# Column sums of the second weight from rows added on GpSimd, and three held steps instead of two at the end of a feed-forward layer

## The chip, the cores and the metric

The kernel runs on one core of a Trainium2 chip. The metric is device time in microseconds (us); lower is better. Engines are named as in the profile: PE (TensorE, matrix products), DVE (VectorE), ACT (ScalarE), POOL (GpSimd) and SP (SyncE, which issues the DMAs).

## The reference

One transformer block for 4 samples of 512 tokens with 512 features. Cross-attention with 32 heads of 16 comes first, then a feed-forward layer whose weights are reduced to three values (-g, 0, g):

```python
x = x + attention(layernorm(x), ctx, ...) @ Wout + bout
def bitlinear(x, w):                       # forward values only
    return einsum('bsd,od->bso', layer_norm(x), sign(round(w / (g + EPS))) * g)   # g = mean(|w|)
h = gelu(bitlinear(layernorm(x), w_fc))    # 512 -> 2048
x = x + bitlinear(h, w_proj)               # 2048 -> 512
```

(The activation quantization changes the value by rounding only.) The second `bitlinear` normalizes each row of `h` before the product. The kernel does it the other way round: it multiplies the unnormalized `h` by the signs W and corrects afterwards. With m the mean and r the inverse deviation of a token's row of `h`,

out = x + r g (h W - m (column sums of W)).

So it needs the column sums of W, one row of 512 numbers: the sum of W over its 2048 rows.

## The kernel before, in words

**Attention** takes the first two thirds of the time. It ends with the last head groups of sample 3. For every second group, a block of 128 rows of `aT` (the attention output) is fetched, and then multiplied on POOL by reciprocals `rb` that went through DRAM (L523, `spread`). The sign chunks of W lie in DRAM; the last four head groups each free two buffers, into which `load_second` (L612) loads two pieces of 256 rows of W. In the end `wproj_sb[f]`, f = 0 to 15, is W as 16 tiles of 128 rows by 512 columns.

**Feed-forward** has 64 steps (sample b, block f of 128 hidden features). The loop over n (L1034) writes the order out by hand for PE, DVE and ACT; POOL and SP are not in that set (L1017), so a scheduler places their instructions. In step n:

- `first(b, f)`, L923: 8 products (4 blocks of features, in a high and a low part) into `hp`, then ACT's Gelu gives `h`.
- `split(b, f)`, L938: ACT rounds `h` to `hh` (L942) and squares it (L953); DVE adds `h` to a running sum (L955), forms the low part `hl` (L956) and adds the squares (L957). All three DVE additions read two tiles of SBUF.
- In steps 6 to 9 of sample 0, the output projection `op` of one tile of 128 tokens of sample 3 (L1047): four products, one for each block k of `aT`.
- In step 7, `column_sums` (L974): 16 products with a matrix of ones (`ones_r`), one for each `wproj_sb[f]`, accumulate the column sums; ACT copies them to `wsum`.
- `second(b, f, t)`, L960, for the four tiles t of 128 tokens, two steps behind `first`: each is a product with `hh` and one with `hl`, 8 in a step.

After the last step of a sample, `totals` (L981) makes 8 small products of the running sums with ones, and a chain of two DVE and six POOL instructions turns them into m and r. For each tile of tokens `centered` (L1003, DVE) subtracts m times the column sums, and `finish` (L1010, DVE) scales by r, adds x and stores.

**The end.** The last two steps of sample 3 are held back: their products are not made step by step but tile by tile (L1096). For t = 0: its 4 products, then `totals`, then `centered(0)`. For t = 1, 2, 3: 4 products, `centered(t)`, `finish(t-1)`. At last `finish(3)`.

Tiles of the feed-forward stage come from `fpool`, opened when attention's pools are closed, so they lie where attention's tiles were, and their first writer waits until those are no longer used.

Of the kernel before, what the change touches and what calls it, by code (L numbers as in the profile page):

```python
# [9 lines left out]
F32 = mybir.dt.float32  # L10
F32R = mybir.dt.float32r
AF = mybir.ActivationFunctionType
ALU = mybir.AluOpType
AX = mybir.AxisListType

P = 128
# [15 lines left out]
def xattn_ffn(  # L32
# [13 lines left out]
    nc = tc.nc  # L46
    B, S, D = x.shape
# [4 lines left out]
    KD, KC, KF = D // P, C // P, F // P  # L52
# [189 lines left out]
    def run(k, end=0):  # L242
        for f in later[end].pop(k, []):
            f()
# [365 lines left out]
    wproj_sb = {}  # L610
# [142 lines left out]
    def when(i, u=0):  # L753
        return burst_of["s", i * NU + u]

    def prepared(b, ready):
        yield [tokens(b, t, ready) for t in range(NT)] + [
            heads(b, n, w) for n in range(2) for w in "kq"
        ] + [values(b, t) for t in range(NT)]
        yield [heads(b, 2, w) for w in "kq"]  # L760
        yield [heads(b, 3, w) for w in "kq"]
# [6 lines left out]
    a, c2, c3 = prepared(2, when(NG))  # L768
    op = projections(0)
    queue += a + op[:2] + c2 + op[2:] + c3  # L770
    a, c2, c3 = prepared(3, when(2 * NG))
# [15 lines left out]
    for k, burst in enumerate(bursts):  # L787
# [72 lines left out]
        while True:  # L860
# [14 lines left out]
            left = open_chore.steps - open_chore.done  # L875
# [13 lines left out]
    left = sorted(later[0].keys() | later[1].keys())  # L889
# [6 lines left out]
    left = sorted(later[1])  # L896
# [13 lines left out]
    fpool = ctx.enter_context(tc.tile_pool(name="fpool", bufs=2))  # L910
# [4 lines left out]

    ones_r = fpool.tile([P, P], F32R, name="ones_r", bufs=1)
    wsum = fpool.tile([P, D], F32, name="wsum", bufs=1)
    hid, parts, acc, fin, outs, opre = {}, {}, {}, {}, {}, {}

    def xbank(name):  # L920
# [2 lines left out]
    def first(b, f):  # L923

        hp = ps_h.tile([P, S], F32, name=f"hp{b}_{f}", tag="h")
        for k in range(KD):
            for half in range(2):
                nc.tensor.matmul(  # L928
                    hp,
                    wfc_sb[k][:, f * P : (f + 1) * P],  # L930
                    dT[b][half][:, k, :],
                    start=half == 0 and k == 0,
                    stop=half == 1 and k == KD - 1,
                )
        hid[b, f] = fpool.tile([P, S], F32, name=f"h{b}_{f}", tag="h", bufs=3)
        nc.scalar.activation(hid[b, f], hp, AF.Gelu, scale=gam_fc[:, 0:1])  # L936

    def split(b, f):  # L938

        x = hid.pop((b, f))  # L940
        high = fpool.tile([P, S], F32R, name=f"hh{b}_{f}", tag="hh", bufs=UB)
        nc.scalar.copy(high, x)  # L942
        low = fpool.tile([P, S], F32R, name=f"hl{b}_{f}", tag="hl", bufs=UB)
        if f == 0:
            acc[b] = [
                fpool.tile([P, S], F32, name=f"acc{n}{b}", tag=f"acc{n}") for n in range(2)
            ]
            nc.scalar.activation(acc[b][1], x, AF.Square)
            nc.vector.tensor_tensor(low, x, high.bitcast(F32), ALU.subtract)
            acc[b].append(x)  # L950
        else:
            sq = fpool.tile([P, S], F32, name=f"sq{b}_{f}", tag="sq")
            nc.scalar.activation(sq, x, AF.Square)  # L953
            old = acc[b].pop() if f == 1 else acc[b][0]
            nc.vector.tensor_tensor(acc[b][0], old, x, ALU.add)  # L955
            nc.vector.tensor_tensor(low, x, high.bitcast(F32), ALU.subtract)  # L956
            nc.vector.tensor_tensor(acc[b][1], acc[b][1], sq, ALU.add)  # L957
        parts[b, f] = (high, low)
# [15 lines left out]
    def column_sums():  # L974

        p = ps_m.tile([P, D], F32, name="wsp", tag="m")
        for f in range(KF):
            nc.tensor.matmul(p, ones_r, wproj_sb[f], start=f == 0, stop=f == KF - 1)  # L978
        nc.scalar.copy(wsum, p)

    def totals(b):  # L981

        p = ps_m.tile([P, 2, NT], F32, name=f"tot{b}", tag="m")
        for n in range(2):
            for t in range(NT):
                nc.tensor.matmul(  # L986
                    p[:, n, t : t + 1],
                    acc[b][n][:, t * P : (t + 1) * P],
                    ones[:, 0:1],
                    start=True,  # L990
                    stop=True,
                )
        m = small.tile([P, 3, NT], F32, name=f"m{b}", tag="m")
        nc.vector.tensor_scalar(m[:, 0, :], p[:, 0, :], -1.0 / F, None, ALU.mult)
        nc.vector.tensor_scalar(m[:, 1, :], p[:, 1, :], 1.0 / F, None, ALU.mult)
        nc.gpsimd.tensor_tensor(m[:, 2, :], m[:, 0, :], m[:, 0, :], ALU.mult)
        nc.gpsimd.tensor_tensor(m[:, 1, :], m[:, 1, :], m[:, 2, :], ALU.subtract)
        nc.gpsimd.tensor_scalar(m[:, 1, :], m[:, 1, :], 0.0, None, ALU.max)  # L998
        r = rstd(m[:, 1, :], 1.0, EPS, NT, f"r_b{b}")
        nc.gpsimd.tensor_tensor(r, r, gam4, ALU.mult)  # L1000
        fin[b] = (m, r)
# [16 lines left out]
    with tc.manual_schedule(engines=ordered):  # L1018
        gam4 = small.tile([P, NT], F32, name="gam4", tag="gam4")
        nc.gpsimd.tensor_scalar(gam4, ones[:, 0:NT], gam_pr[:, 0:1], None, ALU.mult)  # L1020
        steps = [(b, f) for b in range(B) for f in range(KF)]
        todo = list(steps)
        after = {}
        ds = {}
        hold = 0

        def behind(n, f):
            after.setdefault(n, []).append(f)


        for n, s in enumerate(left[1:]):
            behind(2 + n, lambda s=s: run(s, 1))

        for n in range(len(steps) + 4):  # L1034
            on = n < len(steps)
            if on:
                b, f = steps[n]
                first(b, f)
                split(b, f)
                if f == KF - 1 and b + 1 < B:  # L1040
                    behind(n + 1, lambda b=b: totals(b))

            if on and b == 0 and 6 <= f < 6 + NT:
                t = f - 6
                p = xbank(f"op{B - 1}_{t}").rearrange("p k n -> p (k n)")
                for k in range(KD):
                    nc.tensor.matmul(  # L1047
                        p,
                        aT[B - 1][:, k, t * P : (t + 1) * P],
                        wout_sb[:, k, :],  # L1050
                        start=k == 0,
                        stop=k == KD - 1,
                    )
                i = (B - 1) * NT + t
                nc.vector.tensor_tensor(x_sb[:, i, :], p, x_sb[:, i, :], ALU.add)
            if on and b + 1 < B:
                at = (10, 11, 13, 14) if b == 0 else (6, 9, 12, 14)
                for t in range(NT):
                    i = (b + 1) * NT + t
                    if f == at[t] - 4:  # L1060
                        stats(i)
                    elif f == at[t] - 2:
                        ds[i] = prepare(i, fpool, "d")
                    elif f == at[t]:
                        first_T(i, ds.pop(i), xbank(f"tp_d{i}"))()
            if n == 3:
                nc.vector.tensor_copy(ones_r, ones)
            if n == 7:
                column_sums()
            count = 0  # L1070
            while todo and count < 2 and n >= hold:
                sb, sf = todo[0]
                m = sb * KF + sf
                if on and n - m < 2:
                    break
                if sb == B - 1 and sf >= KF - 2:
                    break
                todo.pop(0)
                count += 1
                for t in range(NT):  # L1080
                    second(sb, sf, t)
                if sf == KF - 1:
                    hold = n + 3
                    for t in range(NT):
                        behind(n, lambda b=sb, t=t: centered(b, t))
                        behind(n + 1 + t, lambda b=sb, t=t: finish(b, t))
                    break
            for x in after.pop(n, []):
                x()
            if not on and len(todo) == 2:  # L1090
                break
        for n in sorted(after):
            for x in after[n]:
                x()

        for t in range(NT):  # L1096
            for sb, sf in todo:
                second(sb, sf, t)
            if t == 0:
                totals(B - 1)  # L1100
            centered(B - 1, t)
            if t > 0:
                finish(B - 1, t - 1)
        finish(B - 1, NT - 1)
# [50 lines left out]
```

## Time and profile before

| | us |
|---|---|
| median of 6 runs (lowest to highest) | 857.15 (855.62 to 859.89) |
| the profiled execution: its own time | 857.86 |
| the profiled execution: span from first to last instruction | 856.1 |
| busy: PE, PE weight loads | 813.2, 430.2 |
| busy: DVE, ACT, POOL | 617.9, 456.6, 287.3 |
| mean granted PE clock | 0.991 of full speed |

How to read it: each row of a timeline gives the start, the duration, engine, line, operation, the tile written `<-` the tiles read, sizes and how many instructions were merged. In brackets stands how long the engine was idle before it, and what ended that wait. "PE L928 x8" in the chain of waits is 8 products of line 928 in a row. A column named PEclk is the share of full clock that PE was granted. Line numbers are those of the kernel before.

### The profile page before, as it was taken

How to read it: one execution, taken by the hardware profiler on the slowest of the kernel's cores; microseconds unless marked ns; L12 is line 12 of the kernel's file. 1: busy time of each engine (PE TensorE's matmuls, PEld its weight loads, DVE VectorE, ACT ScalarE, POOL GpSimd, SP SyncE). 2: the span in 40 equal slices, each digit the busy share in tenths (PEclk: the TensorE clock that was granted, in tenths of full speed). 3: DMA queues.
4: the chain of work that ended last, by engine and by line, in shares of the span. 5: the costliest groups of instructions: out<-in, count | busy, mean ns of one | idle time of the engine just before them, and what ended most of it. 6: DMA issues, size and time to landing. Idle time of an engine off the chain costs nothing. (4 is left out here: it accounts for less than half of the span.)

```text
span 856.1 us, 13868 instructions
## 1 busy us (share of the span) xinstructions
PE 813.2 (95%) x5364; PEld 430.2 (50%) x5364; DVE 617.9 (72%) x852; ACT 456.6 (53%) x603; POOL 287.3 (34%) x287
## 2 busy tenths in 40 slices
PE   4599999999999899999999999998999999999996
PEld 2123434344433333433333343336668888888885
DVE  4789878888887988878767877835455864864755
ACT  2245756566664546656555655576234544554442
POOL 3007375553833575577515731301000200100000
PEclk9799999999999999999999999999999999999998
DMA  6885867667596577867644667432000100100101
GB/s 188 280 324 167 264 230 246 219 206 239 196 303 207 184 248 237 293 211 261 210 149 167 230 210 271 150 126 100 1 1 0 50 1 1 50 0 1 50 1 49
DMA packets 75561, 135.25 MB, mean 158 GB/s; under 512 B 10728, under 2 KB 12648, under 8 KB 74984
## 3 DMA queue, kind: packets, MB, share of 16 engines
q1 hardware_dynamic: 75088, 133.72, 46.2%
q8 instruction: 42, 0.69, 0.3%
q10 hardware_dynamic: 408, 0.66, 0.2%
q14 instruction: 23, 0.19, 0.1%
HBM read 79.30 MB, written 55.05 MB: 157 GB/s over the span
## 5 line engine op out<-in xcount | busy, mean ns | idle before, releaser
L437 DVE TENSOR_REDUCE mx<-lp 128x2 f32<-128x1024 f32 x256 | 305.2, 1216 | 85.4 <-PE lp L423 84.6
L474 ACT ACTIVATE es<-sp 128x1024 f32<-128x1024 f32 x256 | 254.4, 1025 | 145.6 <-PE sp L470 137.5
L484 PE MATMUL av<-es,va 128*32 128x512 f32 x1024 | 136.0, 604 | 0.0
L462 PE MATMUL sp<-q_st,k_st 64*128 64x512 f32 x512 | 115.0, 446 | 8.3 <-DVE mx L437 7.5
L423 PE MATMUL lp<-k_st,q_st 64*128 64x512 f32 x512 | 112.7, 437 | 10.2 <-DMA q_st<-q_d 8.2
L936 ACT ACTIVATE h<-hp,gam_fc 128x512 f32<-128x512 f32 x64 | 44.0, 688 | 129.2 <-PE hp L928 129.2
L966 PE MATMUL fp<-wproj,hh 128*128 128x512 f32 x256 | 103.6, 405 | 0.0
L928 PE MATMUL hp<-dTh,wfc 128*128 128x512 f32 x256 | 100.5, 393 | 1.2 <-ACT dTh L657 1.2
L470 PE MATMUL sp<-mrows,sel 64*128 64x512 f32 x512 | 101.1, 391 | 0.2 <-ACT mrows L453 0.2
L966 PE MATMUL fp<-wproj,hl 128*128 128x512 f32 x256 | 101.2, 395 | 0.0
L928 PE MATMUL hp<-dTl,wfc 128*128 128x512 f32 x256 | 100.4, 392 | 0.2 <-DVE dTl L658 0.2
L955 DVE TENSOR_TENSOR acc<-acc,h 128x512 f32<-128x512 f32 x56 | 38.7, 691 | 73.5 <-ACT h L936 73.5
L462 PEld LDWEIGHTS sp<-q_st,k_st 64*128 64x128 f32 x512 | 48.0, 184 | 82.3 <-DVE mx L437 42.4
L423 PEld LDWEIGHTS lp<-k_st,q_st 64*128 64x128 f32 x512 | 48.2, 185 | 81.7 <-ACT es L474 40.9
L523 POOL TENSOR_TENSOR aT<-aT,rb 128x512 f32<-128x512 f32 x16 | 21.2, 1323 | 130.6 <-DMA rb<-rden_d 109.5
L285 PE MATMUL qpq<-xT,wq_sb 128*32 128x512 f32 x512 | 62.3, 594 | 0.7 <-ACT xT L321 0.7
L928 PEld LDWEIGHTS hp<-dTh,wfc 128*128 128x128 f32 x256 | 48.2, 188 | 12.6 <-ACT dTh L657 2.1
L966 PEld LDWEIGHTS fp<-wproj,hl 128*128 128x128 f32 x256 | 48.4, 189 | 11.2 <-issue 0.7
L966 PEld LDWEIGHTS fp<-wproj,hh 128*128 128x128 f32 x256 | 48.3, 189 | 11.2 <-issue 0.7
L928 PEld LDWEIGHTS hp<-dTl,wfc 128*128 128x128 f32 x256 | 48.1, 188 | 11.0 <-DVE dTl L658 0.5
L470 PEld LDWEIGHTS sp<-mrows,sel 64*128 64x128 f32 x512 | 48.4, 186 | 5.9 <-ACT mrows L453 0.8
L196 POOL TENSOR_SCALAR r_a<-mv 128x1 f32<-128x1 f32 x16 | 4.7, 292 | 130.3 <-DVE mv L633 130.3
(129 smaller groups left out, 1038.0 us busy)
## 6 DMA issues: line engine op xcount, KB each, us to landing
k_st<-k_d SPq DMA_DIRECT2D x32, 512.0 KB
q_st<-q_d SPq DMA_DIRECT2D x32, 512.0 KB
k_d<-sh_k SPq DMA_DIRECT2D x32, 256.0 KB
k_d<-sl_k SPq DMA_DIRECT2D x32, 256.0 KB
q_d<-sh_q SPq DMA_DIRECT2D x32, 256.0 KB
q_d<-sl_q SPq DMA_DIRECT2D x32, 256.0 KB
av_d<-avs SPq DMA_DIRECT2D x32, 256.0 KB
wm<-in_wfcT SPq DMA_DIRECT2D x16, 256.0 KB
```

What stands on the lines that cost most here:

```text
L285: nc.tensor.matmul(p[j * HP : (j + 1) * HP, :], w[:, j * HP : (j + 1) * HP], x, start=start, stop=stop,)
L423: nc.tensor.matmul(lp[:, h, :], q_st[i][rows, r, t * P : (t + 1) * P], k_st[i][rows, r, :], start=True, stop=True,)
L437: nc.vector.tensor_reduce(mx[i][:, t, :, r], lp, AX.X, ALU.max, negate=True)
L462: nc.tensor.matmul(sp[:, h, :], k_st[i][rows, r, c * P : (c + 1) * P], q_st[i][rows, r, :], start=True, stop=False,)
L470: nc.tensor.matmul(sp[:, h, :], sel[rows, r, :], mrows[i][rows, :], start=False, stop=True)
L474: nc.scalar.activation(es, sp, AF.Exp, scale=1.0 / math.sqrt(HD))
L484: nc.tensor.matmul(av[j * HP : (j + 1) * HP, :], va[b % 2][:, c, v0 : v0 + HP], es[r][:, h, :], start=c == 0, stop=c == NT - 1,)
L523: nc.gpsimd.tensor_tensor(aT[b][:, n, :], aT[b][:, n, :], rb, ALU.mult)
L928: nc.tensor.matmul(hp, wfc_sb[k][:, f * P : (f + 1) * P], dT[b][half][:, k, :], start=half == 0 and k == 0, stop=half == 1 and k == KD - 1,)
L936: nc.scalar.activation(hid[b, f], hp, AF.Gelu, scale=gam_fc[:, 0:1])
L955: nc.vector.tensor_tensor(acc[b][0], old, x, ALU.add)
L966: nc.tensor.matmul(outs[b][t], parts[b, f][half][:, t * P : (t + 1) * P], wproj_sb[f], start=half == 0 and f == 0, stop=half == 1 and f == ...
```

## The change

Three edits:

1. The 16 products of `column_sums` become one. The 16 tiles of W are first added up on POOL in a new function `add_rows`: 15 additions of 128x512, one behind the other, all into the new tile `wadd`. A single product of ones with `wadd` gives the column sums.
2. `add_rows` is recorded behind step 2 + len(left), where `left` are the leftovers of attention; `column_sums` moves from step 7 to step 12.
3. The last three steps of sample 3 are held back instead of two.

```diff
+    wadd = fpool.tile([P, D], F32R, name="wadd", bufs=1)
...
     def column_sums():
         p = ps_m.tile([P, D], F32, name="wsp", tag="m")
-        for f in range(KF):
-            nc.tensor.matmul(p, ones_r, wproj_sb[f], start=f == 0, stop=f == KF - 1)
+        nc.tensor.matmul(p, ones_r, wadd, start=True, stop=True)
         nc.scalar.copy(wsum, p)
+
+    def add_rows():
+        for f in range(1, KF):
+            a = wproj_sb[0] if f == 1 else wadd
+            nc.gpsimd.tensor_tensor(
+                wadd, a.bitcast(F32), wproj_sb[f].bitcast(F32), ALU.add
+            )
...
         for n, s in enumerate(left[1:]):
             behind(2 + n, lambda s=s: run(s, 1))
+        behind(2 + len(left), add_rows)
...
-            if n == 7:
+            if n == 12:
                 column_sums()
...
-                if sb == B - 1 and sf >= KF - 2:
+                if sb == B - 1 and sf >= KF - 3:
                     break
...
-            if not on and len(todo) == 2:
+            if not on and len(todo) == 3:
                 break
```

The built order of the changed kernel shows where the scheduler puts the new instructions in POOL's queue: eight additions, then the L523 multiply of the third block of `aT`, then seven additions, then the L523 multiply of the fourth block. Behind these come the small r_a instructions of the next sample's normalization. DVE's, ACT's and SP's queues keep their order, but for ACT's copy to `wsum`, which moves with `column_sums`.

## The prediction

> **What bounds the kernel now.** I read the chain of waits first, then its pieces in order of time in the feed-forward stage, then the timelines of POOL, DVE and PE around the edits, then the clock in windows.
>
> The chain's pieces:
>
> ```profile
> 599.23 1.86 PE fp L966 x8
> 601.09 1.81 PE hp L928 x8
> 602.90 3.43 PE op L1047 x8
> 606.33 1.87 PE fp L966 x8
> ...
> 613.49 3.72 PE wsp L978 x16
> ```
>
> Each starts where the one before ended: from 582.66 almost to the end PE is what everything waits for. A product taken off PE is gain, a wait put before one is loss. The 16 products of `column_sums` take 3.72 us, 0.2325 each. The first `op` tile takes 3.43 us, 0.86 for each block of `aT`, so its fourth block is used at 602.90 + 3 x 0.86 = 605.47.
>
> Now POOL and DVE at the start of this stage:
>
> ```profile
> 588.14 1.49 POOL L523 TENSOR_TENSOR aT<-aT,rb 128x512 f32<-128x512 f32 x1 [31.57 <-DMA rb<-rden_d]
> 597.38 1.42 POOL L523 TENSOR_TENSOR aT<-aT,rb 128x512 f32<-128x512 f32 x1 [7.75 <-DMA rb<-rden_d]
> ```
> ```profile
> 587.78 0.69 DVE L956 TENSOR_TENSOR hl<-h,hh 128x512 fp32r<-128x512 f32 x1
> 588.39 1.79 DVE L957 TENSOR_TENSOR acc<-acc,sq 128x512 f32<-128x512 f32 x1
> 590.10 0.68 DVE L955 TENSOR_TENSOR acc<-acc,h 128x512 f32<-128x512 f32 x1
> ```
>
> POOL is idle for long stretches, which makes it look free. But its two multiplies gate PE's `op`, and DVE's addition at 588.39 took 1.79 us, not 0.69. It ended at 590.18, 0.55 us after POOL's multiply ended (588.14 + 1.49 = 589.63). That multiply in turn ended 1.16 us after DVE's addition of 587.78 had (588.47). The second multiply shows the same: POOL ends at 598.80, and an addition of DVE (597.57, 1.78 us) at 599.35. In attention a pair shows it at 305.50: DVE's 1.77 us end at 307.27, 0.56 after POOL's L354, and the next POOL multiply takes 1.73 us and ends 1.15 later. So where both read two tiles of SBUF, **the engines take turns, and a pair costs 1.16 + 0.55 = 1.71 us**. Twice POOL got in ahead of a DVE addition that stood directly behind another one.
>
> **Part 1, the products.** 15 of 16 products go: 15 x 0.2325 = 3.5 us off PE, at a place where PE is the chain. In step 12 PE is the chain as well. ACT's copy to `wsum` moves five steps back in its queue; its first reader is at 667.3, some 25 us behind step 12 (the hp pieces put that step at about 642). It costs nothing.
>
> **Part 2, the additions.** The first waits, by the built order with its waits, for the store of the last attention tile (`avs`), over which `wadd` lies. SP issues that store at 581.42, and the trace has its last landing at 583.46. Alone, dependent POOL instructions of this size follow at 1.36 us (starts 109.52 and 110.88, 1.28 busy). So addition 1 ends at 583.46 + 1.28 = 584.74 and addition 2 at 586.10. At 586.01 DVE's first `hl` comes, and from then on DVE always has an addition waiting: it wants three in each 3.7 us step, one per 1.23 us, and gets one per 1.71. POOL has 15 more instructions until the multiply of the fourth block is done (13 additions, two multiplies): 586.10 + 15 x 1.71 = 611.75. PE needs that block at 605.47. **The wait is 6.3 us, all of it on the chain.** The third block comes seventh among the 15, at 598.1, in time. Its `rb` buffer is then free, and the fourth `rb` lands some 4 us later (issued 593.73, landed 597.2 now), before 611.
>
> DVE's own delay is hidden in this wait. Its n-th turn ends at 586.65 + (n-1) x 1.71: `hl` of step 2 is the sixth (595.2; PE needs it at 595.8), that of step 3 the ninth (600.3 instead of 599.5). PE is 0.9 us late at `op`, whose first three products end at 606.4, and then stands idle to 611.8. If the multiplies were not late, those 0.9 us would be the price. Behind the multiplies POOL's queue holds only r_a, whose inputs come after `op`. The single product in step 12 waits for an addition that ended about 610, so not at all.
>
> **The clock.** An idle PE costs more than its idle time:
>
> ```profile
> 30.00:34.00 4.00, 0.00 (x0) 0.81 0.96 318
> 34.00:37.00 3.00, 0.00 (x0) 0.50 0.89 250
> 37.00:40.00 3.00, 2.84 (x12) 0.50 1.02 311
> 40.00:42.00 2.00, 2.00 (x10) 0.50 1.07 394
> 42.00:44.00 2.00, 1.84 (x14) 0.82 1.06 356
> ```
> ```profile
> 37.16 0.80 PE L423 MATMUL lp<-k_st,q_st 64*128 64x512 f32 x2 [8.23 <-DMA q_st<-q_d]
> ```
>
> These windows give length, PE busy, granted clock, DMA. PE went idle at 37.16 - 8.23 = 28.93. A mean of 0.81 over 30 to 34 puts the fall to half clock at 32.5, 3.55 us later; 0.82 over 42 to 44 puts the return at 42.7, 5.56 us after work began. Half of 5.56 us is lost: 2.8 us. An idle time of 5.4 us (606.4 to 611.8) is longer than 3.55, so I take 2.8. Below it the bound is 0: at 578 to 582 PE was idle for 1.07 and 1.24 us and kept its clock. Above, 5.1, half of the 10.2 us that the fall lasted there.
>
> **Part 3, three held steps.** The end hangs on r_b:
>
> ```profile
> 848.63 0.20 POOL L1000 TENSOR_TENSOR r_b<-r_b,gam 128x4 f32<-128x4 f32 x1
> 848.87 0.75 DVE L1012 SCALAR_TENSOR_TENSOR o<-o,r_b,x_sb 128x512 f32<-128x512 f32 x1 [0.96 <-POOL r_b L1000]
> ...
> 851.51 1.41 DVE L1012 SCALAR_TENSOR_TENSOR o<-o,r_b,x_sb 128x512 f32<-128x512 f32 x2
> ```
>
> Behind r_b six DVE instructions follow without a gap, so the end moves only as `totals` moves, which starts at 844.25. Eight products fewer stand ahead of tile 0 and two more of its own are added, but its last product needs the last `hl`, which ends at 843.72. It starts at 843.77 and `totals` at 844.00: 0.25 us gained. PE stalls over a microsecond for it, and 18 products follow `totals` instead of 12; the last starts at 848.58 - 0.25 + 6 x 0.23 = 849.7 and ends at 850.1, still ahead of its `centered` (850.86 - 0.25). Without that cover of half a microsecond PE would set the end. Bounds: a gain of 0.96 (the whole wait for r_b), a loss of 0.5.
>
> **Sum,** against the profiled execution's own 857.86 (span 856.1 and 1.8 around it): 857.86 + 6.3 + 2.8 - 3.5 - 0.25 = 863.2. The median of the runs shown is 0.7 lower than that execution, so I forecast **862.5**.
>
> **The skill against the rows.** The Trainium skill, "SBUF — State Buffer", section "Who interferes with whom", says that a DVE instruction with two SBUF inputs and a GpSimd instruction that reads SBUF block each other for a whole instruction; this speaks against the change, and the 1.79 us row agrees. "TensorE: Matmul & The Clock Gate", section "What's actually happening", lets the clock rise after about 3.4 us of sustained work, an estimated loss of 1.7 where the row here gives 2.8; by it the sum would be 862.1.
>
> **Rivals.**
> A. *Same wait, the clock stays.* The idle time is shorter than the 8.23 us of the row. 862.5 - 2.8 = 859.7.
> B. *The other side: the additions do not meet DVE* (POOL keeps 1.36 us). 583.46 + 16 x 1.36 + 1.28 = 606.5, a wait of 1.0, no clock fall: 857.86 + 1.0 - 3.5 - 0.25 - 0.7 = 854.4, faster. It decides from a pace under 1.52 us: the fourth block is then done by 609.0 and the wait is no more than the 3.5 saved. For it: 1.28 us is the usual duration of POOL's multiplies. Against: the pairs above, every one with DVE's kind of work from this stage.
> C. *In between, no change* (855.4 to 858.9): DVE runs dry when PE stalls, so that POOL has turns to itself, and the clock stays.
> D. *Longer turns,* the full 1.28 + 0.61 (DVE's usual spacing): 586.10 + 15 x 1.89 = 614.5, a wait of 9.0 and the clock: 865.2; with the clock's upper bound 867.5.
>
> **How the numbers follow.** About 0.2% (1.7 us) is what a measurement of this kernel can tell from no change. Forecast 0.60, A 0.15, B 0.09, C 0.07, D 0.09. Slower: forecast, A and D, 0.84; same 0.07; faster 0.09. The range 858.5 to 866.0 takes in the forecast, A and about half of D, some 0.8; B and most of C lie outside, though the row bounds reach to 854.4 and 867.5.
>
> **What would show it.** Right: POOL's additions near 1.5 us busy with starts 1.7 apart; many DVE additions over 1 us between 586 and 612; the fourth multiply ending near 612, with PE idle before the fourth product of the first `op` tile and PEclk at half for some 5 us afterwards; one `wsp` product without a wait; and `totals` to the end unchanged in length. Wrong: additions at 1.36 us, a full clock, or a PE stall elsewhere than at `op`, such as before `fp`.

## The result, and the profile after

| | before | changed |
|---|---|---|
| median, same measurement (us) | 857.66 (44 runs) | 863.38 (21 runs) |
| ratio, 95% interval | | 1.0069 (1.0058 to 1.0080) |
| profiled execution: time, span | 857.86, 856.1 | 861.99, 860.2 |
| DVE's first `hl` to the end of the last DVE instruction | 266.91 | 273.51 |

The change makes the kernel 0.7% slower, some 5.9 us; 5.35 were forecast (862.5 against the 857.15 shown then). The whole time of an execution spreads over several us (855.27 to 861.33 before), and a profile shows one execution. So I compare profiles over the last row of the table, called **the stretch** below: it holds the feed-forward stage and leaves attention out, where the profiled execution of the changed kernel happened to be 2.45 us faster (first `hl` at 583.56 against 586.01). The stretch is 6.60 us longer.

The chain of waits of the changed kernel, in order of time, from the first addition on (start, duration, what; its lines are some ten further down in the file):

```profile
581.34 1.29 POOL wadd L986
...
582.70 1.30 POOL wadd L986
...
584.08 1.64 POOL wadd L986
...
594.22 1.70 POOL aT L523
...
606.25 1.59 POOL wadd L986
607.85 1.68 POOL aT L523
609.53 0.04 issue
609.57 2.08 PE op L1057 x2
611.65 3.15 PE fp L967 x8
...
646.41 0.23 PE wsp L978
```

Where PE filled the chain before, POOL fills it from 581 to 609.5: additions, a multiply, additions, a multiply. The first two additions, which DVE does not meet, follow each other in 1.36 us; from the third on the pace is 1.70. The row at 594.22 is the multiply of the third block, the one at 607.85 that of the fourth. The PE row `op ... x2` is the two passes of the fourth product. The single `wsp` product takes 0.23 us and waits for nothing.

DVE's timeline beside them:

```profile
586.18 1.77 DVE L957 TENSOR_TENSOR hl<-h,hh 128x512 fp32r<-128x512 f32 x1
587.88 1.78 DVE L958 TENSOR_TENSOR acc<-acc,sq 128x512 f32<-128x512 f32 x1
589.58 1.78 DVE L956 TENSOR_TENSOR acc<-acc,h 128x512 f32<-128x512 f32 x1
```

They start 1.70 us apart and take about 1.77 us each instead of 0.69: the two engines take turns. PE's timeline at the first `op` tile, and the windows there (length, PE busy, PEclk, DMA):

```profile
598.21 0.50 PE L967 MATMUL fp<-wproj,hl 128*128 128x512 f32 x1 [1.10 <-DVE hl L957]
...
601.77 2.73 PE L1057 MATMUL op<-wout_sb,aT 128*128 128x512 f32 x6
609.57 2.08 PE L1057 MATMUL op<-wout_sb,aT 128*128 128x512 f32 x2 [5.07 <-POOL aT L523]
```
```profile
604.00:606.00 2.00, 0.51 (x2) 1.00 0.00 0
606.00:608.00 2.00, 0.00 (x0) 0.88 0.00 0
608.00:610.00 2.00, 0.43 (x1) 0.50 0.00 0
610.00:612.00 2.00, 2.00 (x4) 0.50 0.04 8
612.00:614.00 2.00, 2.00 (x6) 0.50 0.00 0
614.00:616.00 2.00, 2.00 (x9) 0.91 0.00 0
```

Three products (six passes) run, PE stands for 5.07 us, and the clock is at half from 607.5 (mean 0.88 over 606 to 608) to 614.4 (0.91 over 614 to 616). 4.8 us of that fall on work, from 609.57; at half speed that is 2.4 us lost.

The end holds what the prediction did not have. PE's timeline around `totals`, then windows of all engines (PE, PEld, DVE, ACT, POOL busy, then PEclk), and DVE's timeline:

```profile
846.20 0.49 PE L967 MATMUL fp<-wproj,hh 128*128 128x512 f32 x1 [0.49 <-ACT hh L943]
846.93 0.50 PE L967 MATMUL fp<-wproj,hl 128*128 128x512 f32 x1 [0.23 <-DVE hl L957]
847.26 1.84 PE L995 MATMUL tot<-ones,acc 128*128 128x1 f32 x16
```
```profile
847.00:849.00 2.00, 2.00 (x18) 1.96 (x18) 0.47 (x1) 0.00 (x0) 0.00 (x0) 1.00 0.00 0
849.00:851.00 2.00, 2.00 (x8) 1.56 (x9) 0.95 (x3) 0.00 (x0) 1.29 (x5) 0.72 0.00 0
851.00:853.00 2.00, 2.00 (x6) 1.57 (x5) 1.47 (x2) 0.00 (x0) 0.77 (x2) 0.50 0.00 0
853.00:855.00 2.00, 1.96 (x8) 1.25 (x6) 1.40 (x3) 0.00 (x0) 0.00 (x0) 0.93 0.34 131
```
```profile
851.16 0.75 DVE L1014 SCALAR_TENSOR_TENSOR o<-wsum,m,fp 128x512 f32<-128x512 f32 x1 [1.07 <-PE fp L967]
851.88 0.75 DVE L1021 SCALAR_TENSOR_TENSOR o<-o,r_b,x_sb 128x512 f32<-128x512 f32 x1
853.60 0.75 DVE L1014 SCALAR_TENSOR_TENSOR o<-wsum,m,fp 128x512 f32<-128x512 f32 x1 [0.97 <-PE fp L967]
```

The clock falls a second time, 0.8 us after the end of `totals`, for 3.4 us (849.9 to 853.3). The held products run at half speed, and `centered` (L1014) waits for PE where before `finish` waited for r_b. From the last Gelu's start to the end of the last DVE instruction it is 12.26 us instead of 11.26.

So the 6.60 us come from: the fourth product, 26.01 us after the first `hl` instead of 19.46 (+6.55); from there to the last Gelu 235.24 instead of 236.19 us (-0.95, which is -3.5 for the products and +2.4 for the clock, within 0.2); the end (+1.00).

### The profile page after: what moved, and what is told of

Its sections match the earlier page's. It is cut to its first block, busy times and chain, and to the rows that moved or that the text cites. A ratio compares the mean times of both kernels' runs of the same rounds, so it can differ in the third digit from the quotient of the medians.

```text
span 860.2 us, 13867 instructions
## 1 busy us (share of the span) xinstructions
PE 813.3 (95%) x5349; PEld 428.0 (50%) x5349; DVE 630.1 (73%) x852; ACT 456.5 (53%) x603; POOL 312.1 (36%) x302
## 5 line engine op out<-in xcount | busy, mean ns | idle before, releaser
L967 PE MATMUL fp<-wproj,hh 128*128 128x512 f32 x256 | 106.3, 415 | 0.5 <-ACT hh L943 0.5
L967 PE MATMUL fp<-wproj,hl 128*128 128x512 f32 x256 | 103.1, 403 | 1.3 <-DVE hl L957 1.3
L956 DVE TENSOR_TENSOR acc<-acc,h 128x512 f32<-128x512 f32 x56 | 41.7, 745 | 66.9 <-ACT h L937 66.9
L523 POOL TENSOR_TENSOR aT<-aT,rb 128x512 f32<-128x512 f32 x16 | 22.1, 1384 | 92.9 <-DMA rb<-rden_d 89.5
L354 POOL TENSOR_TENSOR oth_k<-oth_k,trig 128x512 f32<-128x512 f32 x14 | 18.0, 1286 | 87.9 <-DVE oth_k L353 87.9
```

Of the source, the lines that this page charges most:

```text
L967: nc.tensor.matmul(outs[b][t], parts[b, f][half][:, t * P : (t + 1) * P], wproj_sb[f], start=half == 0 and f == 0, stop=half == 1 and f == ...
```

## The experiments

Line numbers shift by a few from kernel to kernel. The ratios are against runs of the kernel before on the same chip, with 95% intervals; the stretch is that of the one profile.

| kernel | ratio | stretch | last Gelu to end |
|---|---|---|---|
| before | 1 | 266.91 | 11.26 |
| changed | 1.0069 (1.0058 to 1.0080) | 273.51 | 12.26 |
| three held steps alone | 1.0012 (0.9998 to 1.0025) | 266.79 | 11.14 |
| the same, second profile | single run | 267.91 | 12.27 |
| additions, two held steps | 1.0067 (1.0048 to 1.0086) | 272.70 | 11.27 |
| changed, PE filled at `op` | 1.0054 (1.0035 to 1.0072) | 270.20 | 11.13 |
| changed, memsets for additions | single run | 263.33 | 11.14 |
| no additions, two held | 0.9959 (0.9935 to 0.9983) | 263.50 | 11.28 |
| POOL by hand, two held | 0.9963 (0.9946 to 0.9980) | 263.95 | 11.28 |
| additions spread, two held | 1.0026 (1.0009 to 1.0043) | 268.15 | 11.28 |

**My theory** after the result: the slowdown is the queue ahead of the fourth multiply, stretched by the turns, plus the clock's fall, less the products. **Rivals:** the three held steps cost it; DVE's late parts cost it, not the queue; the clock's fall is only a sight, because other engines set the pace meanwhile.

### The parts by themselves

The third edit alone, put on the kernel before:

```diff
-                if sb == B - 1 and sf >= KF - 2:
+                if sb == B - 1 and sf >= KF - 3:
...
-            if not on and len(todo) == 2:
+            if not on and len(todo) == 3:
```

> The kernel before with three held steps instead of two and nothing else. The prediction's working of the end: totals 0.25 us earlier, DVE's chain behind it unchanged, so 0.25 us faster, and the stretch from the last Gelu to the last DVE instruction 11.0 us instead of 11.26. Rival, from the profile of the changed kernel: PE's waits for hh and hl ahead of totals (0.49 and 0.23 us) and the small products of totals leave PE idle enough that its clock falls to half for some 3 us in the held products, centered then waits for PE, and the stretch is 12.2 us: some 1.0 us slower. A fall that depends on the moment would show in some executions only.

Measured: a ratio of 1.0012, which cannot be told from no change. The profile kept its clock at the end, and 11.14 us is a gain of 0.12, not 0.25. PE's windows there (length, PE busy, PEclk, DMA):

```profile
847.00:849.00 2.00, 2.00 (x11) 1.00 0.00 0
849.00:851.00 2.00, 1.75 (x8) 1.00 0.07 27
```

A second profile:

> The kernel before with three held steps once more, for a second profile of its end. If the clock's fall there depends on the moment, either 11.1 us from the last Gelu to the last DVE instruction with the clock kept, as in its first profile, or 12.2 us with the clock at half among the held products, as in the changed kernel's; other lengths would need another cause.

Measured: 12.27 us, with the clock at half from 848.7 to 852.1. PE's windows of that second profile:

```profile
847.00:849.00 2.00, 2.00 (x12) 0.93 0.00 0
849.00:851.00 2.00, 2.00 (x6) 0.50 0.00 0
851.00:853.00 2.00, 2.00 (x8) 0.71 0.34 131
```

So one kernel shows both ends, and the fall depends on the moment. Of the five profiles with three held steps (the changed kernel, these two, the filled PE and the memsets below) two show it, of the five with two held steps none.

The changed kernel with the third edit undone:

```diff
-                if sb == B - 1 and sf >= KF - 3:
+                if sb == B - 1 and sf >= KF - 2:
```

> The changed kernel with two held steps: the additions and the single product alone. If the additions cost what the sum says (a wait of 6.3 to 6.6 us, 2.4 to 2.8 for the clock, 3.5 saved), 5.2 to 5.9 us slower than before. If the three held steps cost 1 us, this is 1 us faster than the changed kernel; if they gain 0.25 us, it is 0.25 slower. From the last Gelu to the last DVE instruction 11.26 us as before.

Measured: 1.0067, and a stretch 5.79 us longer than before. The slowdown is that of the additions; the held steps are not needed for it.

The additions away as well:

```diff
-        behind(2 + len(left), add_rows)
...
-        nc.tensor.matmul(p, ones_r, wadd, start=True, stop=True)
+        nc.tensor.matmul(p, ones_r, wproj_sb[0], start=True, stop=True)
```

> The changed kernel with two held steps and without the 15 additions; the one product reads the first 128 rows of W alone, so the column sums are left out of the output. It shows what 15 fewer products are worth by themselves. The sum says 3.5 us faster than before (15 x 0.2325), also in the stretch from DVE's first hl to the last DVE instruction (266.9 before, 263.4 here). Rival, that the products' time is given back at another wait later on: less than 2 us faster.

Measured: 0.9959 (3.5 us, 1.5 to 5.6), and the stretch 3.41 us shorter. The products are worth what the sum said, and nothing of it is given back later.

### The wait at op: queue, turns and clock

22 products more, where PE stands:

```diff
                 for k in range(KD):
+                    if t == 0 and k == KD - 1:
+                        fill_p = ps_m.tile([P, D], F32, name="fill", tag="m")
+                        for j in range(22):
+                            nc.tensor.matmul(
+                                fill_p, ones_r, wproj_sb[0], start=j == 0, stop=j == 21
+                            )
                     nc.tensor.matmul(
```

> The changed kernel with 22 more products on PE (5.1 us, into a bank that nobody reads) ahead of the fourth product of the first op tile, where PE stands idle. If the clock's fall is a cost of its own: the fourth product starts at the same 26.0 us after DVE's first hl, the clock stays at full speed behind it, and the time is some 2.4 us below the changed kernel's (about 3.3 above before). Rival, the fall costs nothing because other engines set the pace there: the same time as the changed kernel.

```profile
602.48 2.73 PE L1063 MATMUL op<-wout_sb,aT 128*128 128x512 f32 x6
604.65 5.69 PE L1060 MATMUL fill<-wproj,ones_r 128*128 128x512 f32 x22
610.38 1.12 PE L1063 MATMUL op<-wout_sb,aT 128*128 128x512 f32 x2
```

```profile
606.00:608.00 2.00, 2.00 (x10) 1.00 0.00 0
608.00:610.00 2.00, 2.00 (x11) 1.00 0.00 0
610.00:612.00 2.00, 1.96 (x7) 1.00 0.00 0
```

These are PE's timeline and three of its windows. The fourth product comes 26.10 us after the first `hl` (584.28), as in the changed kernel, but the clock is full in every window from 602 to 614. From the fourth product to the last Gelu (843.35) it takes 232.97 us against 235.24: **2.27 us are the clock's**, with the same wait and with more work on PE. The whole times (1.0054 against 1.0069) point the same way, but their intervals overlap.

Memsets in place of the additions:

```diff
-            nc.gpsimd.tensor_tensor(
-                wadd, a.bitcast(F32), wproj_sb[f].bitcast(F32), ALU.add
-            )
+            for _ in range(2):
+                nc.gpsimd.memset(wadd.bitcast(F32), float(f))
```

> The changed kernel with each of POOL's 15 additions replaced by two memsets of the same tile, which read nothing (so the column sums are left out, and the output differs by them). If DVE and POOL take turns only when both read SBUF: DVE's additions take 0.69 us beside the memsets (0.53 us each), and the fourth multiply ends some 20 us after POOL's first instruction (28.2 in the changed kernel), before PE needs it; no PE wait at op, 3.5 us faster than before in that stretch. Rival, any work on POOL slows DVE, or the queue alone is the delay: DVE's additions above 1 us, or PE's wait stays above 3 us.

POOL's and DVE's timelines:

```profile
589.29 1.33 POOL L523 TENSOR_TENSOR aT<-aT,rb 128x512 f32<-128x512 f32 x1
590.56 8.12 POOL L986 MEMSET wadd<- 128x512 f32 x14
598.64 1.75 POOL L523 TENSOR_TENSOR aT<-aT,rb 128x512 f32<-128x512 f32 x1
```
```profile
589.38 1.78 DVE L958 TENSOR_TENSOR acc<-acc,sq 128x512 f32<-128x512 f32 x1
591.09 0.68 DVE L956 TENSOR_TENSOR acc<-acc,h 128x512 f32<-128x512 f32 x1
591.69 0.68 DVE L957 TENSOR_TENSOR hl<-h,hh 128x512 fp32r<-128x512 f32 x1
```

DVE's addition takes 1.78 us beside POOL's multiply and 0.68 beside the memsets. So what holds DVE here is not that POOL is busy, but that it reads (or computes from) two tiles; the run does not separate these two. On the queue this run says less than it was meant to: the scheduler put only 22 of the 30 memsets ahead of the fourth multiply, which ended 15.7 us after the first memset, in time; the stretch is 3.58 us shorter than before.

POOL's order written by hand, so that both multiplies come first:

```diff
-    ordered = {mybir.EngineType.PE, mybir.EngineType.DVE, mybir.EngineType.Activation}
+    ordered = {
+        mybir.EngineType.PE,
+        mybir.EngineType.DVE,
+        mybir.EngineType.Activation,
+        mybir.EngineType.Pool,
+    }
```

> The changed kernel with two held steps and POOL's order in the feed-forward stage as it is recorded: both multiplies of aT first, then all 15 additions, then the small r_a instructions. If the queue ahead of the fourth multiply is the cost, PE's wait at op is gone and the clock stays. The additions then run from about 599 for 15 x 1.71 = 25.7 us, and r_a of the next sample, needed by DVE for prepare in step 8 some 8 us before their end, waits behind them: DVE stands still for up to 7 us, of which PE's lead over hl covers some 4 to 5. So between 3.5 and 0.5 us faster than before. Rival, taking turns alone is the cost (late hl parts, not the queue): as slow as the changed kernel.

```profile
597.09 1.79 POOL L523 TENSOR_TENSOR aT<-aT,rb 128x512 f32<-128x512 f32 x1 [7.39 <-DMA rb<-rden_d]
598.84 1.29 POOL L986 TENSOR_TENSOR wadd<-wproj 128x512 fp32r<-128x512 f32 x1
600.20 22.94 POOL L986 TENSOR_TENSOR wadd<-wadd,wproj 128x512 fp32r<-128x512 f32 x14
```

Measured: 0.9963 (3.2 us faster, 1.7 to 4.6), the stretch 2.96 us shorter. The same 15 additions take turns with DVE here too (22.94 us for 14, 1.64 each) and cost 0.45 us (263.95 against 263.50 without any). DVE stood 1.5 us for r_a and PE only 0.27 us. The kernel with the additions and two held steps (1.0067) differs from this one in POOL's order alone. So turns alone are not the cost; **it is what queues behind them.** This version beats both kernels.

The additions spread over the steps:

```diff
-        behind(2 + len(left), add_rows)
+        for f in range(1, KF):
+            behind(4 + (f - 1) * 11 // 15, lambda f=f: add_rows([f]))
...
-            if n == 12:
+            if n == 16:
                 column_sums()
```

> As the kernel with POOL's order by hand, but with the additions spread: one or two behind each of the steps 4 to 14, and the single product in step 16. No queue of more than two additions stands ahead of a multiply or an r_a, and DVE loses at most 2 x 1.16 us in a step of 3.7 in which it needs 1.9. Expected 3.3 to 3.5 us faster than before, equal to the kernel without additions. Rival, that DVE's turns make hl late even so: PE waits ahead of fp, and less than 2 us faster.

A miss: 1.0026, the stretch 1.24 us longer than before. POOL's, then DVE's, then PE's timeline:

```profile
637.02 9.44 POOL L984 TENSOR_TENSOR wadd<-wadd,wproj 128x512 fp32r<-128x512 f32 x6
```
```profile
645.23 1.78 DVE L956 TENSOR_TENSOR acc<-acc,h 128x512 f32<-128x512 f32 x1
```
```profile
648.86 0.66 PE L653 MATMUL tp_d<-ident,d 128*128 128x128 f32 x4 [2.01 <-DVE dTl L658]
```

In this order the additions stand behind the r_a of their step, and r_a waits for DVE's statistics; POOL stood idle for 11.3 us before one of them. Six additions then came in a row in steps where DVE has `prepare` and `dTl` to do besides, DVE became late, and PE waited 2.01 us. `totals` waited 0.34 us more for the `wsum` copy, which I had put right ahead of it in the same bank, and the clock fell for 3.4 us at 661.8 (1.7 lost). These three come to 4.05 us; less the 3.5 of the products they make 0.55 of the 1.24 us, and 0.7 us stay unassigned.

## Why the prediction was right or wrong

- **The wait.** Right, in mechanism and size: 6.55 us for 6.3, a pace of 1.70 for 1.71, the third block 12.36 us after the first `hl` for 12.1, PE's earlier wait for the `hl` of step 3 1.10 for 0.9. The order by hand shows that the place in POOL's queue makes it a cost.
- **The clock.** Right in kind, over by a little: 2.4 us by the windows and 2.27 by the filler run, for 2.8. It fell 3.0 us after PE stopped (604.5 to 607.5) and came back 4.8 us after work resumed, for 3.55 and 5.56 in the row I took. These are not fixed lengths. In each of the ten profiles all changes of the clock lie on one grid of 3.41 us, and the grid lies differently in each. Here it cuts at 604.1, 607.5, 610.9 and 614.4: the clock fell at the end of an interval in which PE worked for 0.4 us, and came back at the end of the first that PE filled. In the row I took, too, it came back after the first filled interval (39.3 to 42.7), and in the kernel with two held steps 5.3 us after the same wait. So how much a stop costs depends on where the grid lies, and how near 2.8 came is partly luck. Rival A, the clock stays, was not seen behind this wait. The Trainium skill ("TensorE: Matmul & The Clock Gate", section "What's actually happening") lets the clock rise after at least one busy window of about 3.4 us. The trace agrees on the filled interval (610.9 to 614.4). Counted from the moment work resumes, as the prediction did, 3.4 us would be an estimated loss of 1.7; the 4.8 us measured make 2.4, between that and the row.
- **The products.** Right: 3.41 by themselves, for 3.5.
- **The three held steps.** This step failed: "the end moves only as `totals` moves" held only where the clock was kept. There the gain was 0.12 to 0.13 us for 0.25, because `totals` came 2.46 us after the last Gelu's start instead of 2.59: the product behind the last `hl` held it for 0.34 us, not 0.23. The term missing was a clock fall at the end, which in two of five profiles made the end 1.0 us longer than before. I had priced PE's stall there (over a microsecond, I thought; measured 0.49 and 0.23 us) as covered by DVE and put the clock behind it at nothing, though I had just priced one. The bound of 0.5 for a loss was too small.
- **The sum.** In the profiles the whole is 6.60 us for 5.35. The wait is 0.25 more than forecast, the products and the clock together 0.25 less, and the end 1.25 more. The first two cancel by chance, and the error left is the end's. How many of the executions without a profile have the fall at the end is not known.
- **The rivals.** B (no turns, 1.36 us) is ruled out by the starts 1.70 apart, D (1.89) too, and C (no change) by the measured ratio. (One of the three pairs named against B, the one at 305.50, is not of this stage but of attention; the other two are.)

What sets off the fall at the end can be read from the same grid, though it is a reading of rows and not an experiment. In the changed kernel the interval that ends with the fall (846.46 to 849.88) holds all 16 small passes of `totals` and the wait of 0.23 us; the large products keep PE busy for 1.64 us of it. In the second profile with three held steps it is 1.77 us (845.32 to 848.73, `totals` and a part of that wait), and ahead of the fall at 661.8 in the spread version 1.27. In every other interval of the ten profiles that holds passes of `totals` it is at least 1.86 us, and the clock stays. In the three profiles with three held steps that kept the clock, a cut of the grid lies between the last wait and most of `totals` (in the first, both waits end by 844.27 and the cut is at 844.41). So by these rows it takes `totals` and a wait in the same interval, and what differs from execution to execution is where the grid lies.

## What to carry to other kernels

An engine that is idle half the time is not free: look at what stands behind the new work in its queue, and whether its neighbour must share with it. Let the built order tell where the scheduler put it; here putting POOL among the engines ordered by hand turned 0.7% slower into 0.4% faster with the same additions. And when PE is the chain, price an idle time on it twice, once for itself and once for the clock after it.

## What the runs showed of the hardware that was not expected

- A DVE instruction with one SBUF input can be held too: the 128x128 cast of `ones_r` took 0.22 us before and 1.32 beside the additions. Its row in the changed kernel:

```profile
599.78 1.32 DVE L1077 CAST ones_r<-ones 128x128 fp32r<-128x128 f32 x1
```

- The turns were strict: DVE was never idle from 586 to 609 in the changed kernel, so its next addition stood ready, and still it never got two long turns in a row between two POOL instructions (only a short one-input instruction and then an addition).
- PE's clock was low for 3.41, 6.83 or 10.24 us at a time in all ten profiles, except where a run ended in it: one, two or three steps of the grid.
- The clock can fall without PE being idle for 3.41 us: at the end of the changed kernel it fell after waits of 0.49 and 0.23 us and the small products of `totals`.
